# Selective scans: states summed by sixteen 32x32 tiles into four banks that y shares with the projection's scratch

## The chip, the core and the metric

The kernel runs on one core of a Trainium2 chip. The time is that of the whole program on the device, in microseconds (us). The kernel before takes 9509.47 us, the median of three runs (9506.33 to 9523.89).

## What is computed

Two layers of a "metaformer" on an input of 4 x 64 x 64 x 128, all in float32. Each layer adds a token mixer and then a channel mixer to x, each behind a layer norm. The change is in the token mixer of the second layer, a selective scan in four directions k over each image of L = 4096 positions, with 256 channels d (two halves of 128, called h) and 16 states n:

```
x_dbl = einsum('bkdl,kcd->bkcl', xs, x_proj_w)        # 8 rows for dt, 16 for B, 16 for C
dt = softplus(einsum('bkrl,kdr->bkdl', dts_r, dt_proj_w) + dt_proj_b)
h = h * exp(dt * A) + (dt * u) * B                     # for each position l, channel d, state n
y = einsum('bkdn,bkn->bkd', h, C)                      # the sum over the states
ys = ys + Ds * xs
y = ys[0] + ys[2] reversed + transposed(ys[1] + ys[3] reversed)
```

Directions 0 and 2 walk the rows of the image forward and backward, 1 and 3 the columns. After the scans y is normalized, gated and projected to 128 channels.

## The kernel before

The program runs its stages one after the other: attention, a recurrent layer solved by sweeps, the inputs of the scans (in_proj, a 3x3 convolution by 32x32 tiles at L950), the scans (L998 to L1485), their outputs, and a mixture of experts. Only the scans and the order of some weights are touched by the change.

**Windows, groups, tiles.** A sequence is cut into blocks of 125 positions. Four blocks make a window of W = 500 positions; there are 33 windows for each direction, 132 in all, walked in the order k = 2, 3, 0, 1. A window has four groups q of four states each, a group has a tile for each block. A tile holds 128 channels by two halves h by four states by 127 columns, 1016 columns in all. One DVE instruction scans a tile (L1297). There are 16 tiles in a window and 2112 scans.

**A step p of the schedule.** The order is written out by hand (the loop over p at the end of the function). In step p PE fills the addend db of tile p + 1 (L1273: eight matmuls of 32 rows that multiply dt * u by B into one of two double banks), ACT carries the last column of the states of tile p - 1 into the decays of the next tile of its group (L1318), DVE scans tile p, PE sums the states of a group that is done (L1348, at even p: two of four n each time), POOL multiplies the states of tile p by C (L1331) into a ring of twelve products, SP loads C for tile p + 5 (L1250), ACT computes exponentials of dt * A for coming groups (L1238), and one or two pieces of the projection of a coming window are put in.

**The projection** (`project`) is a generator whose pieces are tied to steps, from 40 to 10 steps ahead of its window. It has a scratch `mm` in PSUM, two banks, and uses it one after the other for: x_proj (L1142) and its copy xd (L1147); dt_proj (L1161), exp (L1172), a bound (L1175, L1177), ln (L1181) and the maximum that gives dt (L1186); the transposes of B (L1194), which DVE spreads on diagonals (b_diag, L1200); the transposes of dt * u (L1221), which ACT copies to dtu_t (L1223).

**y.** The sum over states is taken by PE: an identity of 64x64 times the products, for row halves r and channel halves h, four tiles of 64x64 with 500 columns that run together (L1348). Row half r goes to bank r, so y has two banks; in them partition 64 h + c, bank r stands for channel 128 h + 64 r + c. `add_other` (L1359) adds, by the same tiles, D * u in the backward directions and the y of the backward direction in the forward ones; k = 3 has nothing to add. `finish` (L1369) copies y on ACT, and SP writes it out. While y is open, each fill puts a matmul with zeros beside its pairs, into y, on a row group of 32 that the fill leaves idle (L1282, called a filler here): it adds nothing to y.

In the order of the halves that y has, the weights of the stages after it are laid out with channels exchanged (`turned`).

## Time and profile before

| | |
|---|---|
| median of three runs | 9509.47 us |
| the profiled execution | 9517.0 us |
| its span | 9515.2 us |
| scans, first to last start of L1297 | 3598 to 8847 us of the span |
| DVE scan L1297 | 2112 times, 4669.3 us busy |
| POOL products L1331 | 2112 times, 4457.4 us busy |
| ACT exponentials L1238 | 4224 times, 3017.5 us busy |
| PE sums L1348 | 16896 records of 64x500, 2019.2 us busy |
| granted PE clock in the scans, 4500 to 8700 us | 1.00 |

The page gives the busy time of each engine as a share of the span: PE is TensorE's matmuls (in float32 each matmul of the program is two records), PEld its weight loads, DVE VectorE, ACT ScalarE, POOL GpSimd, SP the queue that issues DMAs. Below stand groups of instructions by source line with their count, busy time and the mean of one, and then the idle time before them with the engine that ended it ("<-PE y L1348"). A timeline line has the start in us of the span, the time that the merged instructions took, engine, line, operation, result and operand, shapes and count. Matmuls that run together on different tiles of the array overlap in it.

### The profile page before, as it was taken

The page shows a single profiled execution, that of the slowest core. Times are in us where ns is not written, and L with a number is a line of the kernel's source. Part 1 is how long each engine was busy: PE and PEld are TensorE (multiplying, and loading weights), DVE is VectorE, ACT ScalarE, POOL GpSimd, SP SyncE. Part 2 cuts the span into 40 slices and gives each one's busy share as a digit, 9 for nine tenths or more (in the row PEclk, how much of TensorE's full clock was granted, in tenths as well). Part 3 has the DMA queues.
Part 4 walks back from the last instruction along what each step waited for, and adds up shares of the span by engine and source line. Part 5 has one row for each costly group of instructions (what it writes and reads, how often), then busy time and mean ns, then how long its engine had stood idle before and what let it go on. Part 6 is the DMA issues. An engine that isn't in the chain of part 4 may idle for free. (4 is left out here: it accounts for less than half of the span.)

```text
span 9515.2 us, 237518 instructions
## 1 busy us (share of the span) xinstructions
PE 8735.5 (92%) x102194; PEld 4329.6 (46%) x102194; DVE 8414.2 (88%) x5099; ACT 6880.6 (72%) x10398; POOL 5155.1 (54%) x2433
## 2 busy tenths in 40 slices
PE   7999999999988978999999999999999999999766
PEld 3333333333333335555555555555555555555223
DVE  6999999999978218999999999999999999999764
ACT  3888888888855457777777877877777777777321
POOL 0000000000001018999999999999999999999100
PEclk8999999999999988999999999999999999999887
DMA  4000000000011325666666556666666666666634
GB/s 171 31 8 34 10 8 35 8 8 10 8 60 62 123 121 156 170 171 171 170 167 160 160 160 158 160 168 171 171 171 171 171 170 171 171 171 165 228 116 182
DMA packets 530960, 1164.75 MB, mean 122 GB/s; under 512 B 76818, under 2 KB 444506, under 8 KB 502106
## 3 DMA queue, kind: packets, MB, share of 16 engines
q1 hardware_dynamic: 529882, 1149.30, 41.6%
q8 instruction: 807, 13.22, 0.6%
q14 instruction: 271, 2.22, 0.1%
HBM read 828.51 MB, written 182.15 MB: 106 GB/s over the span
## 5 line engine op out<-in xcount | busy, mean ns | idle before, releaser
L1297 DVE TENSOR_TENSOR_SCAN states<-decays,db 128x1016 f32<-128x1016 f32 x2112 | 4669.3, 2256 | 100.8 <-ACT decays L1318 61.5
L1331 POOL TENSOR_TENSOR products<-states,c_ring 128x1000 f32<-128x1000 f32 x2112 | 4457.4, 2152 | 219.9 <-PE y L1348 190.2
L1238 ACT ACTIVATE decays<-dt,a_logs 128x500 f32<-128x500 f32 x4224 | 3017.5, 714 | 90.4 <-DVE states L1297 4.2
L1273 PEld LDWEIGHTS db<-b_diag,dtu_t 32*128 32x128 f32 x16896 | 2051.3, 187 | 1607.0 <-DVE states L1297 1186.4
L1273 PE MATMUL db<-b_diag,dtu_t 32*128 32x128 f32 x16896 | 2429.8, 283 | 316.0 <-DVE states L1297 310.2
L1273 PE MATMUL db<-b_other,dtu_t 32*128 32x128 f32 x16896 | 2458.9, 284 | 0.0
L1282 PE MATMUL y<-zeros 32*128 32x128 f32 x14720 | 2122.4, 283 | 0.0
L1273 PEld LDWEIGHTS db<-b_other,dtu_t 32*128 32x128 f32 x16896 | 2050.1, 186 | 0.3 <-issue 0.2
L1348 PE MATMUL y<-products,ident 64*64 64x500 f32 x16896 | 2019.2, 592 | 1.1 <-POOL products L1331 1.1
L1282 PEld LDWEIGHTS y<-zeros 32*128 32x128 f32 x14720 | 1772.1, 186 | 0.0
L341 DVE TENSOR_TENSOR total<-total,ring 128x2048 f32<-128x2048 f32 x768 | 1706.9, 2285 | 32.5 <-ACT ring L303 31.8
masks.py:197 POOL MEMSET ident<- 128x128 f32 x6 | 1.2, 204 | 2915.1 <-SPq L180 2623.1
L303 ACT ACTIVATE ring<-sa 128x2048 f32<-128x2048 f32 (+3 forms) x667 | 1153.5, 1738 | 274.2 <-PE sa L288 262.6
L313 PE MATMUL av<-ring,v_at 128*32 128x256 f32 (+1 forms) x16128 | 1095.9, 388 | 6.2 <-ACT o L322 5.7
L1348 PEld LDWEIGHTS y<-products,ident 64*64 64x64 f32 x16896 | 541.3, 132 | 696.8 <-issue 568.3
L313 PEld LDWEIGHTS av<-ring,v_at 128*32 128x32 f32 x16128 | 421.4, 109 | 951.0 <-issue 749.0
L303 ACT ACTIVATE ring<-sb 128x1536 f32<-128x1536 f32 (+2 forms) x585 | 800.5, 1375 | 73.8 <-PE sb L288 63.9
L1318 ACT COPY decays<-states 128x8 f32<-128x8 f32 x2048 | 405.2, 198 | 536.3 <-DVE states L1297 520.0
L288 PE MATMUL sa<-q_at,k_at 32*128 32x512 f32 x4898 | 701.4, 641 | 20.3 <-issue 14.1
L288 PE MATMUL sb<-q_at,k_at 32*128 32x512 f32 x3294 | 624.1, 641 | 0.0
L288 PEld LDWEIGHTS sa<-q_at,k_at 32*128 32x128 f32 x4898 | 192.5, 183 | 354.4 <-issue 176.9
L338 DVE TENSOR_TENSOR total<-ring 128x2048 f32<-128x2048 f32 x128 | 288.6, 2287 | 66.7 <-ACT ring L303 66.4
(211 smaller groups left out, 7955.5 us busy)
## 6 DMA issues: line engine op xcount, KB each, us to landing
c_ring<-c_rows SPq DMA_DIRECT2D x2112, 250.0 KB, 4.6
b_other<-b_diag SPq DMA_DIRECT2D x264, 512.0 KB, 6.5
weights<-in_w SPq DMA_DIRECT2D x32, 1024.0 KB, 12.9
u<-u_r SPq DMA_DIRECT2D x60, 500.0 KB, 5.6
y_r<-sum SPq DMA_DIRECT2D x60, 500.0 KB, 4.2
u<-u_c SPq DMA_DIRECT2D x60, 500.0 KB, 5.7
y_c<-sum SPq DMA_DIRECT2D x60, 500.0 KB, 4.2
x<-x SPq DMA_DIRECT2D x96, 256.0 KB, 2.6
```

The lines of the kernel that those rows point to most:

```text
L288: nc.tensor.matmul(s[:, m, :], k[rows, tokens(t)], q[rows, chunk(chunk_state["c"])], start=True, stop=True,)
L303: nc.scalar.activation(ring[:, lo : lo + n, :], s[:, at : at + n, :], AF.Exp)
L313: nc.tensor.matmul(chunk_state["av"][rows, some], chunk_state["v"][:, t, rows], ring[:, at + i, some], start=t == 0, stop=t == NJ - 1 and ...
L338: nc.vector.tensor_add(total, sums[g - 2], w)
L341: nc.vector.tensor_add(sums[g % 2], sums[g % 2], w)
L1238: nc.scalar.activation(to, dt, AF.Exp, scale=scale)
L1273: nc.tensor.matmul(bank.rearrange("p (n t) -> p n t", n=4)[:, :, to : to + 32], v.dtu[rows, h, s, :], b[rows, s, 4 * self.q : 4 * self.q + ...
L1282: nc.tensor.matmul(y[:, idle // 2, :P], zeros[rows], zeros[rows], start=False, stop=False)
L1297: nc.vector.tensor_tensor_scan(order(self.slot(states)), order(self.slot(decays, shift)), order(self.db[:, SKIP + shift :][:, : 2 * LANE]) ...
L1318: nc.scalar.copy(self.edge(later.slot(decays), later.v.into), last)
L1331: nc.gpsimd.tensor_mul(to, h, c)
L1348: nc.tensor.matmul(to, ident[rows, rows], of, start=begins, stop=ends)
```

## The change

The sums, `add_other` and the layout of y go from 64x64 to 32x32 tiles: row groups r of 32 products rows, and column groups 2 h + j, where j is the half of the window (250 positions). Row group r writes bank r, so y now has four banks, 250 columns in each; partition 32 (2 h + j) + c, bank r stands for channel 128 h + 32 r + c. A block of sums has 32 matmuls of 250 columns instead of 8 of 500.

The scratch mm no longer has banks of its own: y is columns 0 to 249 and mm columns 256 to 511 of the same four banks (the two double banks of db hold the other four). The matmuls into mm no longer start a group of their own; they add onto places that ACT has set to zero. So three copies of zeros are put on ACT in each window's projection (`cleared`: after xd, after b_diag, after dtu_t; a fourth for the first two windows only), and the transposes become matmuls with an identity. x_proj and dt_proj are cut in two halves of 250 columns; dt_proj takes 64 rows of a weight tile that is zero beyond the 9 that matter. The fillers write into y as before, now into bank 1 or 2, that of their row group.

y is written to memory in natural channel order, by four DMAs for each piece of a window instead of one, and read back as `other` by one instead of four; the exchanged channel order of weights and norm goes away.

```diff
-    mm = ps.tile([P, ND, CH], F32, tag="mm", name="mm", bufs=1)
+    ym = ps.tile([P, 4, CH], F32, tag="ym", name="ym", bufs=1)
+    nc.vector.memset(ym, 0.0)
+    y, mm = ym[:, :, :WH], ym[:, :, CH // 2 :]
+    wide = mm[:, :, :WH]
+
+    def cleared(of):
+        nc.scalar.copy(of, zeros[:, 0:1].rearrange("p (r o) -> p r o", o=1).to_broadcast(list(of.shape)))
...
     def project(v):
...
-            nc.tensor.matmul(
-                x_ps[:, :W], w_x[:, h, k, :], v.u[:, h, :], start=h == 0, stop=h == ND - 1
-            )
+            for j in range(2):
+                nc.tensor.matmul(
+                    wide[:, 2 + j],
+                    w_x[:, h, k, :],
+                    v.u[:, h, j * WH : (j + 1) * WH],
+                    start=False,
+                    stop=h == ND - 1,
+                    skip_group_check=True,
+                )
...
+        cleared(wide[:, 2:])
...
         yield -17
+        if v in todo[:2]:
+            cleared(wide)
...
         yield -12
+        cleared(mm[:, 1:2, : NS * N])
...
         yield -10
-        nc.scalar.copy(v.dtu, turned)
+        nc.scalar.copy(v.dtu.rearrange("p h (j s) d -> p (h j) (s d)", j=2), mm)
+        yield -9
+        cleared(mm)
...
                     nc.tensor.matmul(
-                        y[:, idle // 2, :P], zeros[rows], zeros[rows], start=False, stop=False
+                        y[:, idle, :P],
+                        zeros[rows],
+                        zeros[rows],
...
+    def to_y(r, h, j):
+        c = 32 * (2 * h + j)
+        return y[c : c + 32, r, :]
+
+    def each_tile():
+
+        for r in range(4):
+            for h in range(ND):
+                for j in range(2):
+                    yield r, h, j
...
     def sum_of(pair, n):
...
-        for r in range(2):
-            rows = slice(HALF * r, HALF * r + HALF)
-            for h, g in enumerate(pair):
-                y = v.y[HALF * h : HALF * h + HALF, r, :W]
-                begins = q == 0 and n == 0
-                ends = q == Q - 1 and n == 3
-                of, to = window_of(products, rows, g, n, v.data.start, y)
-                nc.tensor.matmul(to, ident[rows, rows], of, start=begins, stop=ends)
+        for r, h, j in each_tile():
+            rows = slice(32 * r, 32 * r + 32)
+            of, to = window_of(
+                products, rows, pair[h], n, v.data.start, to_y(r, h, j), (2 * j, 2 * j + 1)
+            )
+            nc.tensor.matmul(
+                to,
+                ident32[rows],
+                of,
+                start=q == 0 and n == 0,
+                stop=q == Q - 1 and n == 3,
+                skip_group_check=True,
+            )
...
     def finish(v):
-        v.sum = work.tile([P, ND, W], F32, tag="sum", name="sum", bufs=1)
-        nc.scalar.copy(v.sum, v.y[:, :, :W])
+        v.sum = work.tile([P, 4, WH], F32, tag="sum", name="sum", bufs=1)
+        nc.scalar.copy(v.sum, y)
         for b, of, to in v.pieces:
-            nc.sync.dma_start(ys[b][v.k % 2][:, :, of], v.sum[:, :, to])
+            for j in range(2):
...
+                for h in range(ND):
+                    c = 32 * (2 * h + j)
+                    nc.sync.dma_start(
+                        ys[b][v.k % 2][:, h, at : at + end - first].rearrange(
+                            "(r c) t -> c r t", r=4
+                        ),
+                        v.sum[c : c + 32, :, first - j * WH : end - j * WH],
+                    )
```

## The prediction

> **What bounds the kernel now.** I read the page's first two parts, the busy time by stretch, the waits, and then one window of sixteen scans in the timelines of DVE, PE and ACT. Only the scans (3598 to 8856 us of the span) are touched.

> ```profile
> PE 8735.5 (92%) x102194; PEld 4329.6 (46%) x102194; DVE 8414.2 (88%) x5099; ACT 6880.6 (72%) x10398; POOL 5155.1 (54%) x2433
> 5500.00:6500.00 1000.00, 937.41 (x13125) 554.93 (x13124) 976.94 (x511) 792.88 (x1493) 969.59 (x458) 1.00 0.61 162
> POOL products L1331 <- PE y L1348: 143.3, 101, 1.7
> ACT sum L1369 <- PE y L1348: 120.6, 96, 1.9
> DVE dt L1186 <- POOL low L1177: 49.8, 100, 0.5
> DVE states L1297 <- ACT decays L1318: 42.2, 69, 1.0
> DVE states L1297 <- PE db L1273: 19.3, 100, 1.6
> ```

> The page makes PE the busiest. The second line (busy us of PE, PEld, DVE, ACT, POOL in 1000 us of scans) says that DVE, with 977, is the one with nothing left; PE's 937 holds fillers and modelled ends. The waits (us in total over 4000 to 8000, times, longest) show the small rest: three short waits of DVE, each in up to all of the 101 windows there, two of which begin with PE's sums L1348 (ACT's copy of y and POOL wait for them).

> ```profile
> 8537.62 13.15 DVE L1297 TENSOR_TENSOR_SCAN states<-decays,db 128x1016 f32<-128x1016 f32 x6
> 8551.38 4.48 DVE L1297 TENSOR_TENSOR_SCAN states<-decays,db 128x1016 f32<-128x1016 f32 x2 [0.62 <-ACT decays L1318]
> 8556.02 4.43 DVE L1297 TENSOR_TENSOR_SCAN states<-decays,db 128x1016 f32<-128x1016 f32 x2 [0.16 <-PE db L1273]
> 8560.95 0.68 DVE L1186 TENSOR_TENSOR dt<-mm,low 128x500 f32<-128x500 f32 x1 [0.50 <-POOL low L1177]
> ...
> 8577.50 13.15 DVE L1297 TENSOR_TENSOR_SCAN states<-decays,db 128x1016 f32<-128x1016 f32 x6
> ```

> Six scans back to back take 13.15 us, a step of (13.15 - 2.26) / 5 = 2.18. The window is 8577.50 - 8537.62 = 39.88. DVE's own work is 16 x 2.18 + two b_diag (1.15, 1.12 by their steps) + two dt (0.6) = 38.3. So only 1.5 us of a window is waiting: all that a faster PE can give back. By every sixteenth scan the windows take 39.9 in direction k=2, 39.2 in k=3 (no added other, L1359), 39.87 in k=0 and 1.

> **The change, part by part.** *The sums.* Now eight 64x64 matmuls, after it thirty-two 32x32 ones of half the columns.

> ```profile
> 6002.64 1.91 PE L1348 MATMUL y<-products,ident 64*64 64x500 f32 x16
> 6004.48 0.37 PE L1273 MATMUL db<-b_diag,dtu_t 32*128 32x128 f32 x1
> 3322.64 9.66 PE L950 MATMUL conv_ps<-xin,diag 32*32 32x512 f32 x286
> ```

> A block of sums holds PE for 6004.48 - 6002.64 = 1.84 us: 4 rounds of 0.42 (each matmul is two records of 500 columns; four tiles run together) and about 0.15 to switch tiles. The nearest row for sixteen 32x32 tiles is the convolution's: 9 taps in 9.66 us, less its last record's 0.6, is 1.0 us for each sixteen matmuls of about 507 columns; two passes at the sums' pace would be 0.85, so sixteen tiles cost about 0.17 more than their columns. For 250 columns: 2 x (0.42 + 0.17) + 0.1 = 1.28. [...] I take 1.25, near the row. PE is freed of 1056 x 0.59 = 620 us, and the added other shrinks by some 0.4 us in three windows of four. Against DVE's floor this can bring at most 1.5 us x 98 + 0.9 x 33 = 180 us.

> *The shared banks.* y takes columns 0 to 249 of four banks, the projection's scratch columns 256 to 511 of the same four. Before, mm and y had banks of their own, so ACT's copies from mm ran beside PE's fillers (L1282 writes y): the trace has them overlapping at no price. [...] PE takes matmuls in the program's order, so a waiting filler holds up all of PE behind it: the rest of its own fill, for which the next scan waits, then sums and projections. [...]

> *The clears.* Three copies of zeros on ACT per window, of 500, 64 and 1024 columns. Nearest rows: quarters 128x512 at 0.63, the carry L1318 at 0.2, dtu_t 128x1024 at 0.99. Together 1.85 us; ACT goes from 79% to about 84%. Off the path that is free; where a filler or a carry stands behind it, it is not (bounds: 0 if all is covered, 1.85 if none).

> ```profile
> 8543.63 0.99 ACT L1223 COPY dtu_t<-mm 128x1024 f32<-128x1024 f32 x1
> 8550.20 0.99 ACT L1369 COPY sum<-y 128x1000 f32<-128x1000 f32 x1 [1.48 <-PE y L1348]
> 8553.41 0.99 ACT L1172 ACTIVATE e<-mm 128x1000 f32<-128x1000 f32 x1
> 8554.52 1.04 ACT L1175 ACTIVATE low<-e 128x1000 f32<-128x1000 f32 x1
> ```

> *One window.* Slots are p modulo 16, time 0 is slot 0's scan; a fill takes 1.1 on PE (from 6004.48 its last records start at 6005.38, eight rounds of 0.11), and 0.85 from a released filler to its end (6 rounds and the last matmuls; 0.75 to 1.1), then 0.14 to the scan; decays take 0.74 each, a carry 0.2.
> - The first b_diag waited for a matmul ahead of the sums, now for the sums: fill 0.3 to 1.4, sums to 2.65, so 2.7 for 2.2: 0.5 lost.
> - xd (0.68) and its clear (0.63) follow b_diag, to 5.25; the filler goes at 5.3, the fill ends at 6.15, and the second b_diag now waits for it: 6.3 for 6.05, 0.25.
> - dtu_t now waits for the sums' end at 14.3 and ends at 15.3; fill to 16.2; slot 6's scan 16.35 for 16.15: 0.2.
> - ACT does a carry, two decays, then clears 1024 columns, to 18.0; filler, fill to 18.9, slot 7's scan 19.05 for 18.5: 0.55.
> - Three decays to 20.4, the copy of y to 21.4, the carry to 21.6; slot 8's scan 21.7 for 21.2: 0.5 (it is 0.6 to 0.7 now: the sums are no longer late, ACT is).
> - Three decays and the carry to 24.0; slot 9's scan 24.1 for 23.9: 0.2.
> - L1172 waited for w_dt's matmuls, now for the sums after them, at 24.65; exp, its reading, L1175 and the carry end at 26.9; slot 10's scan 27.0 for 26.3: 0.7.
> - dt no longer waits for POOL, but its second half waits for sums: 0.1.

> That is 3.0 us of waiting for 1.5, a window of 41.35. With the other added nothing changes, its 0.6 us ends before the clear does. Sum: 98 x (41.35 - 39.89) + 33 x (41.35 - 39.2) = 143 + 71 = 214 us. POOL (38.3 us of work in a window) stays below 41.35.

> *Small edits.* y goes out by four DMAs per piece for one, in runs of 1000 for 2000 bytes, and other comes in by one for four in k=0 and 1. The issues (0.56 us of SP each in the trace) stand before c_ring loads, which are put out five slots (12 us) ahead and land in 4.6: covered; without cover 3 x 0.56 per window in k=2, at most 55 us. w_dt with 64 rows for 9, w_x in halves, transposes as matmuls with an identity: the same columns through PE. Memsets and the clears before the first scan: about 6 us (0 to 15). Channel order costs nothing.

> The profiled execution took 9517.0 us (span 9515.2), 7.5 above the median of 9509.5. 9517 + 214 + 6 = 9737; against the median, 9730.

> **Rivals.** *Waiting doubles* (above), 9730, chance 0.68: for it the program's waits and DVE at 98%. [...] *Issue limits the sums*: a block of 2.1 makes those four steps 0.85 later each, 44.75 per window, 9509 + 131 x 5 = about 10170; chance 0.08; against it, bursts of three tiles start 7 ns apart in the fills. In between lie blocks of 1.5: +1 us, 9860. *PE was the bound and is freed, so it is faster*: if fillers are released within about 0.4 us of a fill's start, the waits L1348 causes go and no new ones come; DVE's floor of 38.3 gives up to 180 us, 9330; the wait counts of POOL and ACT on y speak for it, the nine waiting fillers against; chance 0.06. The rest, 0.04, is that the copies pass one another better than I laid out, within 0.2%.

> The range is 9540 to 9890: below it lie the faster case and the overlapping one, above it the issue limit, some 0.18 in all. 0.2% (19 us) is what a measurement tells from no change: faster 0.06, within 0.07, slower 0.87.

> **What will show it.** Right: L1369's successor and L1172 ended by PE y; fillers (L1282's) that idle for ACT; a window near 41.4; a block of sums of 1.2 to 1.35 us; DVE's share at 93%. DVE's waits should be named PE db and ACT decays, at slots 2, 6 to 10. Wrong: windows below 39.9, a block under 1.0 or above 1.8, a granted clock below 1.00 in the scans, or POOL waiting for c_ring.

## The result, and the profile after

The changed kernel takes 12818.5 us (median of four runs, 12758 to 12868), the kernel before 9514.1 us beside it: 1.347 times as long, 95% interval 1.339 to 1.355. The prediction was 9730 us, at most 9890. Its sign was right, its size wrong by 3090 us. The profiled execution of after has a span of 12864.0 us. Its busy times, its granted clock in 40 slices, and the stretch of scans that was shown of before:

```profile
PE 11458.5 (89%) x157898; PEld 7085.2 (55%) x157898; DVE 8534.2 (66%) x5099; ACT 7144.9 (56%) x10796; POOL 5202.1 (40%) x2433
...
PEclk8999999999866666666555555666666666666687
```

```profile
5500.00:6500.00 1000.00, 885.40 (x14316) 656.65 (x14284) 608.71 (x308) 514.48 (x958) 594.49 (x278) 0.62 0.39 100
```

DVE, which had 977 us of work in 1000, now has 609: it waits. PE is still busy for 885, but at a granted clock of 0.62 (the third number from the end), where before had 1.00. The PEclk row shows that this sets in with the scans and ends with them. Every sixteenth scan (131 distances) is 65.35 us apart on average, where before had 39.79: 25.56 x 131 = 3348 us, the whole difference of the two spans (12864.0 - 9515.2).

What the engines waited for, 4000 to 8000 us of after (us in total, times, longest):

```profile
DVE states L1346 <- PE db L1317: 1076.4, 591, 3.3
...
ACT e L1196 <- PE ym L1405: 301.8, 61, 5.0
ACT dtu_t L1266 <- PE ym L1405: 261.4, 61, 5.0
...
PE ym L1326 <- ACT ym L1075: 196.0, 121, 2.2
```

The first line was 19.3 us in before. Fillers (L1326) wait for ACT, as predicted. But look at who waited for the sums in the whole span. First before, all of it, then after (us, times):

```profile
who waited for it (us, times):
  POOL products L1331: 190.2, 130
  ACT sum L1369: 172.7, 125
```

```profile
who waited for it (us, times):
  POOL products L1380: 1045.4, 390
  ACT e L1196: 638.9, 130
  ACT dtu_t L1266: 558.9, 130
  ACT ym L1075: 453.4, 130
  DVE b_diag L1235: 325.3, 130
  DVE dt L1210: 289.8, 130
  ACT sum L1433: 285.9, 132
```

Five readers and clears of the projection's scratch, once in each window, stand behind blocks of sums from which they take nothing: they share their banks. One such place, in the order of start (the last brackets hold the idle time before the instruction and what ended it; L1196 is the exp that reads dt_proj's result):

```profile
7781.11 2.34 PE L1405 MATMUL ym<-products,ident 32*32 32x250 f32 x64
7781.32 2.27 DVE L1346 TENSOR_TENSOR_SCAN states<-decays,db 128x1016 f32<-128x1016 f32 x1 [1.70 <-PE db L1317]
...
7783.49 1.00 ACT L1196 ACTIVATE e<-ym 128x1000 f32<-128x1000 f32 x1 [4.95 <-PE ym L1405]
...
7784.63 0.57 PE L1326 MATMUL ym<-zeros 32*128 32x128 f32 x1 [0.46 <-ACT e L1196]
...
7786.45 2.27 DVE L1346 TENSOR_TENSOR_SCAN states<-decays,db 128x1016 f32<-128x1016 f32 x1 [2.85 <-PE db L1317]
```

Block of sums, reader, filler with the rest of its fill, scan: four links one after the other, 5.3 us from 7781.11 to 7786.45, for a step that takes 2.2 when nothing waits. And each PE link is long: the block takes 2.34 where at full clock it takes 1.47.

### The profile page after: what moved, and what is told of

The parts are those of the page before. It is cut to its first block, busy times and chain, and to the rows that moved or that the text cites. A ratio compares the mean times of both kernels' runs of the same rounds, so it can differ in the third digit from the quotient of the medians.

```text
span 12864.0 us, 349349 instructions
## 1 busy us (share of the span) xinstructions
PE 11458.5 (89%) x157898; PEld 7085.2 (55%) x157898; DVE 8534.2 (66%) x5099; ACT 7144.9 (56%) x10796; POOL 5202.1 (40%) x2433
## 5 line engine op out<-in xcount | busy, mean ns | idle before, releaser
L1326 PE MATMUL ym<-zeros 32*128 32x128 f32 x14720 | 3267.9, 387 | 925.2 <-ACT ym L1075 406.6
L1317 PE MATMUL db<-b_diag,dtu_t 32*128 32x128 f32 x16896 | 3978.7, 394 | 12.8 <-DVE states L1346 10.3
L1317 PE MATMUL db<-b_other,dtu_t 32*128 32x128 f32 x16896 | 3974.2, 394 | 0.0
L1317 PEld LDWEIGHTS db<-b_diag,dtu_t 32*128 32x128 f32 x16896 | 3267.4, 279 | 999.2 <-issue 759.0
L1326 PEld LDWEIGHTS ym<-zeros 32*128 32x128 f32 x14720 | 2790.4, 279 | 1180.5 <-ACT ym L1075 456.2
L1317 PEld LDWEIGHTS db<-b_other,dtu_t 32*128 32x128 f32 x16896 | 3263.0, 279 | 0.0
L1405 PE MATMUL ym<-products,ident 32*32 32x250 f32 x67584 | 2217.3, 555 | 0.3 <-POOL products L1380 0.3
L1405 PEld LDWEIGHTS ym<-products,ident 32*32 32x32 f32 x67584 | 1030.6, 128 | 607.0 <-issue 362.9
L288 PE MATMUL sa<-q_at,k_at 32*128 32x512 f32 x4898 | 701.4, 640 | 20.4 <-issue 14.1
L1235 DVE TENSOR_TENSOR b_diag<-ym,ident 128x1024 f32<-128x1024 f32 x264 | 323.2, 1224 | 424.9 <-PE ym L1405 325.3
L1210 DVE TENSOR_TENSOR dt<-ym,low 128x500 f32<-128x500 f32 x264 | 178.9, 678 | 629.3 <-PE ym L1326 311.0
```

What stands on the lines that cost most here:

```text
L288: nc.tensor.matmul(s[:, m, :], k[rows, tokens(t)], q[rows, chunk(chunk_state["c"])], start=True, stop=True,)
L1235: nc.vector.tensor_mul(v.b_diag[:, i : i + 2].rearrange("p s n t -> p (s n) t"), b_ps[:, i : i + 2] .rearrange("p s (n o) -> p (s n) o", o ...
L1317: nc.tensor.matmul(bank.rearrange("p (n t) -> p n t", n=4)[:, :, to : to + 32], v.dtu[rows, h, s, :], b[rows, s, 4 * self.q : 4 * self.q + ...
L1326: nc.tensor.matmul(y[:, idle, :P], zeros[rows], zeros[rows], start=False, stop=False, skip_group_check=True,)
L1405: nc.tensor.matmul(to, ident32[rows], of, start=q == 0 and n == 0, stop=q == Q - 1 and n == 3, skip_group_check=True,)
```

## The experiments

Two things had to be told apart: new waits, and a low clock. The trace records the granted clock as 1.00 or as 0.50, which is called half clock here. "Window" is the mean distance of every sixteenth scan, "half" the share of time in the scans at half clock, both over 111 windows (10 to 120, counted from 0). "Work" is what I counted in each trace: the columns that each matmul streams, times its share of the array's rows and columns, in 3.41 us (4096 would be the whole array at full clock without a break: eight records of 128x512, which start 0.43 us apart at full clock and 0.85 at half, L118 of before). "Idle" is PE's longest idle time there. Work is not independent of the clock: at half clock PE streams half as many columns in the same time (125 columns of the sums take 0.41 us at full clock and 0.83 at half, E11 below). E1, E3, E4 and E11 were run once, the others twice or more.

```
kernel                                   us      window  work  PE busy  idle  half
before                                  9514.1    39.7   2721   0.94    1.7   0.00
E4 before, no fillers                   9528.4    39.8   2407   0.94    1.7   0.01
E1 before, half sums                    9406.0    39.0   2116   0.84    3.2   0.08
E7 before, half sums, no fillers       11376.1    53.9   1301   0.98    1.0   0.91
E6 before, fillers in scratch           9777.7    41.8   2654   0.94    1.5   0.03
E8 the same, half sums                  9600.4    40.6   2104   0.91    1.5   0.16
E16 as E6, light ties                  11367.5    54.0   2060   0.89    1.6   0.20
E17 as E8, light ties                  11507.2    54.6   1568   0.90    1.6   0.52
after                                  12818.5    65.6   1312   0.89    2.2   0.76
E2 after, two fillers                  11049.3    51.5   1908   0.84    2.2   0.25
E3 after, no fillers                   11767.0    57.0   1293   0.94    2.7   0.78
E10 after, fillers where they are free 10739.7    49.3   1673   0.89    3.6   0.40
E9 after, sums of 32x64                12159.8    59.8   1894   0.87    2.2   0.28
```

### The clock: E1 to E4, E7

The first theory, A, was that the clock follows the work done in the array: half sums and waits leave too little. Its rival B: idle PE behind the new waits trips it.

E1 is before, with sums of two blocks of four:

```diff
-                nc.tensor.matmul(to, ident[rows, rows], of, start=begins, stop=ends)
+                half = slice(0, NB) if begins else slice(2 * (n % 2), 2 * (n % 2) + 2)
+                nc.tensor.matmul(
+                    to[:, half],
+                    ident[rows, rows],
+                    of[:, half],
...
```

> The kernel before, with its own banks for mm and y, but each sum L1348 takes only two of the four blocks (250 of 500 columns; the first one of a window takes all), so part of y is left out: PE's useful work per block is halved as in the change, with no new wait anywhere. Theory A (the granted clock follows how much of the array works within a 3.4 us stretch: columns x rows x columns of the tile): a pair of slots brings 1536 from fills and 1000 from sums for 2000, so the clock falls in some stretches: mean clock in the scans 0.80 to 0.98, 9450 to 10500 us. Theory B (PE standing still behind the new waits lets the clock fall; less work alone does not): clock 1.00 and 9330 to 9500 us.

E2 is after with a second filler in each place; E3 and E4 are after and before without any (`if False:` for the filler's condition).

```diff
-                if summed[-1]:
-                    rows = slice(32 * idle, 32 * idle + 32)
+                for r in (idle, (idle + 2) % 4) if summed[-1] else ():
+                    rows = slice(32 * r, 32 * r + 32)
                     nc.tensor.matmul(
-                        y[:, idle, :P],
+                        y[:, r, :P],
...
```

> The changed kernel with a second filler beside the first, in the fourth row group that a fill leaves idle: the waits are all there, a fill brings 1024 instead of 768 of array work. Theory A: the clock comes back to 0.95 to 1.00 in the scans, and the slots run as the prediction laid them out: 9620 to 9850 us. Theory B (idle time behind waits): the gaps are as long as before, so the clock stays at 0.6 and the time at 12500 to 13100.

> The changed kernel without any filler: fills no longer wait for ACT or DVE in their middle, and there is less array work. Theory A: half clock nearly throughout (0.50 to 0.58 in the scans); fills of 1.7, sums of 2.3 and the projection give some 54 to 62 us per window, 11400 to 12500 us, so PE's pace at half clock is the bound. Theory B: the gaps go with the waits, the clock is back above 0.9, 9400 to 9900 us.

> The kernel before without its fillers. Theory A: a pair of slots still brings 1024 + 2000, in the poorest 3.4 us about 2000, above the some 1450 where the clock changed in the changed kernel's trace: clock 1.00, 9480 to 9560 us. Rival (the fillers themselves hold the clock, because they keep a further row group busy at all times): the clock falls below 0.8 and the time is over 10500.

E1 took 9406.0 us, E2 11049.3 (ratio 1.161, 1.158 to 1.165), E3 11767.0, E4 9528.4. B's numbers fail for E2 and E3: more work beside the same waits raised the clock and saved 1770 us; the fillers' waits removed, work with them, left it low. A has the times of E3 and E4 right and E2 wrong: E2 has 1908 of work, a clock mostly full, and still windows of 51.5. E1 fell between the two, A's clock at B's time. It also answers what a shorter block is worth without sharing: 1.1% less time than before in one run. Its 51 windows (of all 131) without half clock take 38.31 us on average, DVE's own 38.3.

E7 joins E1 and E4: half sums, no fillers, no new wait.

> Before with the sums of 250 of 500 columns (part of y is left out) and without fillers: the array work of a window is the same as in the changed kernel without fillers (some 1770 columns of the whole array in 3.4 us if a window takes 40 us), but no wait is new. Theory W: clock 0.85 to 1.00 in the scans, windows of 38.3 to 41 us, 9350 to 9650 us. Rival C: the clock falls as in the changed kernel without fillers (0.6), windows above 44 us, over 10200 us.

11376.1 us (1.196; 1.193 to 1.200), the line of C, the rival that held the array work alone to be enough. The stretch 5500 to 6500 of E7, of E1 and of E4:

```profile
5500.00:6500.00 1000.00, 979.54 (x7736) 681.06 (x7734) 747.60 (x384) 606.42 (x1130) 736.43 (x344) 0.54 0.46 119
```

```profile
5500.00:6500.00 1000.00, 833.86 (x13259) 582.73 (x13251) 977.16 (x515) 803.39 (x1510) 978.37 (x462) 0.96 0.63 165
```

```profile
5500.00:6500.00 1000.00, 935.52 (x10268) 547.47 (x10264) 973.60 (x509) 793.12 (x1494) 966.61 (x457) 0.99 0.61 161
```

PE is busy for 980 of 1000 us in E7 and has a clock of 0.54; in E1 it is busy for 834 and has 0.96. So PE's busy time alone is not what the clock goes by here. Either cut of work alone keeps it; both together lose it. The low clock then thins the work further, by an estimate: at half clock E7's windows take 54 us, so its 20566 units of work a window come to 1301 in 3.41 us, while in windows of 39.8 they would be 1760.

### The waits: E5, E6, E8, E10

E6 brings into before one thing of the change: the fillers go into the scratch. (dt_proj also takes 64 rows, with zeros, as in after; so it is in E8 and E14 to E17.)

```diff
-                        y[:, idle // 2, :P], zeros[rows], zeros[rows], start=False, stop=False
+                        mm[:, idle % 2, :P], zeros[rows], zeros[rows], start=False, stop=False,
...
```

With fillers among the values under way in the scratch, E6's output is off by a relative 0.031; E8 and E14 to E17 have them there too.

> Before, with one thing of the change alone: the fillers write into the projection's scratch (the bank that matches after's) in place of y's banks, so that they wait for ACT and DVE as in after, while the sums stay 64x64 and the array work of a window stays what it was (the dt projection takes 64 rows with zeros in place of 25 so that the tiles can stand beside each other). Theory W: the scans get late, windows of 42 to 48 us, PE has empty stretches but 64x64 sums around them, clock 0.85 to 1.00, 9850 to 10900 us. The size of waits in the prediction (3 us a window in place of 1.5): windows of 41 to 41.5 us at clock 1.00, 9700 to 9780 us. Rival C: clock 1.00, since the array work is there. If the empty stretches alone hold the clock down: clock below 0.8 and over 11000 us.

> Before with two things of the change and nothing else: the sums of 250 of 500 columns (part of y is left out; array work of a window as in after) and the fillers in the projection's scratch (waits as in after). Alone the first gave 9406 us and the second 9778 us. Theory I (the clock is decided by the array work per stretch of 3.4 us, so that less work and new waits, each harmless alone, together put many stretches below the threshold, and the low clock then holds itself): clock in the scans below 0.85, windows above 46 us, 10500 to 12500 us. Rival S (the two add up, and the rest of after's time is of the 32x32 tiles or the clears): 9406 - 9509 + 9778, about 9675 us, clock above 0.93, 9550 to 9900 us.

E6 took 9777.7 us (1.028; 1.025 to 1.031). Its 84 windows (of all 131) without half clock are 41.22 us on average: what the prediction had for the whole change, and below theory W's 42 to 48. E8, with half sums too, took 9600.4 (1.010; 1.007 to 1.013): rival S has its time right, the two nearly add up (9675), and theory I, that their meeting is enough, falls. Less work and waiting fillers do not make after.

E5 and E10 take the waiting fillers out of after and double the others. This is E10's list of places:

```diff
+                late = self.p % 16 in (0, 4, 5, 6, 8, 9, 12, 13, 15)
+                for r in (idle, (idle + 2) % 4) if summed[-1] and not late else ():
...
```

> After, with no filler in the nine fills per window whose first filler was seen to wait (tiles 2, 3, 4, 6, 7, 10, 11, 13, 14 of 16) and two fillers in each of the other seven. No part of the computation changes: fillers add zeros. Theory W (the waits of the fillers behind the shared banks make the scans late and leave PE empty; the empty stretches bring the clock down, and the low clock then does the rest): windows of 16 scans from 42 to 46 us, clock in the scans above 0.9, 9850 to 10450 us. Rival C (the clock goes by the average array work alone, and the sums' half work is what is missing): the nine bare fills are like those of the kernel without fillers, clock 0.55 to 0.7 in the scans, windows of 53 to 57 us, 11300 to 11900 us.

> After, with two fillers in each fill whose first filler did not wait, and none in the nine of 16 where it did. The earlier kernel of this kind took the places in the order of the fills for the tiles' numbers, which are two higher, and so left most waits in; here the numbers are right. Theory I: the fillers' waits are gone, but nine fills hold no filler: the average is some 2070 columns of the whole array in 3.4 us at windows of 40 us, between the kernel that fell (1770) and the one that mostly held (2115): clock 0.75 to 0.97, windows of 40 to 50 us, 9600 to 11000 us. Rival: the waits of the fillers are not what delays the scans, and the time stays where the earlier one was, above 11200 us.

E5 took 11319.4 us (1.190) and tells little: its list was of places in the order of fills, two below the tiles' numbers, so most waits stayed. E10 took 10739.7 us (1.130; 1.126 to 1.133), within theory I's range and the best of after's kin, and still 1230 us above before: with no filler that waits, its windows with 0.2 to 0.3 of half clock are 47.0 us.

### The sums' own sharing: E9, E12 to E17

E9 gives the sums of after their array work back.

```diff
+    nc.vector.tensor_copy(padded[:, 32:64], ident32)
...
-                ident32[rows],
+                padded[rows, 32 - 32 * j : 96 - 32 * j],
```

> After with its sums by tiles of 32 rows x 64 columns: the identity has 32 zero columns beside it, so that each matmul also adds zeros to the other half's partitions. Nothing of the computation changes; the array work of the sums is that of before again (2000 columns of the whole array a block in place of 1000), their instructions, banks, clears and waits are after's. Theory I: the clock is back at 0.93 or above in the scans, and what remains is the waits at full clock and a block near before's 1.84 us: windows 41.5 to 46 us, 9750 to 10450 us. Rival T (the many small instructions, not their array work, bring the clock down): clock below 0.8, over 11500 us.

12159.8 us (1.279; 1.275 to 1.283) at a clock of 0.87. Theory I missed the time, and its rival T, whose time it is, missed the clock: most of the clock came back, the time did not. With PE busy for only 0.87 and DVE for two thirds (2973 of 4500 us), this is waiting; its block is 2.27 us, and readers that stand behind it wait longer.

So theory Q: readers wait for blocks of sums, fillers for readers. E12 issues the projection ahead of the sums in after, E13 in E10.

```diff
             if p in at:
                 at[p].scan()
+            projections(p)
             sums(p)
...
-            projections(p)
```

> After, with the projection's steps of a turn issued ahead of the turn's sums in place of behind them. Nothing of the computation changes. Theory Q (both ways of the sharing make a chain: the projection's reader on ACT or DVE waits for a whole block of sums that was issued ahead of it in its banks, and the next fill's first filler waits for the reader, so that block, reader and fill follow each other; the low clock comes of the PE time lost and stretches each link): the readers no longer stand behind the block, though the block now stands behind the reader: windows of 44 to 57 us, clock 0.65 to 0.95, 10200 to 11800 us. Rival C (the array work decides, the order of issue matters little): 12500 to 13100 us.

> The same swap in the kernel that has two fillers in the seven fills that did not wait and none in the nine others (10740 us without the swap, windows of 47 to 51 us). Theory Q: of the two sides of the chain one is shortened and the other gone: windows of 41 to 47 us, 9700 to 10650 us. Rival C: no change within 150 us of 10740.

E12: 12095.3 us (1.272), 720 below after, but above Q's range and below C's; E13: 11554.3 us (1.215), 815 above E10, where Q expected a gain. The swap turns the wait round: the sums then wait for readers and clears, 432 us in E12 from 4000 to 8000 us, where after has no such wait. The largest of these in E12:

```profile
PE ym L1405 <- ACT ym L1075: 198.4, 132, 2.7
```

Neither of the two orders of issue gets rid of it.

E14 to E17 leave before as it is and tie its sums to the scratch: a small matmul of zeros into each bank of the scratch, ahead of each block and behind it. In E14 and E15 it has 128x128 and 32 columns, in E16 and E17 64x64 and 4 columns.

```diff
+        def tie():
+            for bank in range(ND):
+                nc.tensor.matmul(
+                    mm[:HALF, bank, :4], zeros[:HALF, :HALF], zeros[:HALF, :4],
+                    start=False, stop=False,
...
+                tie()
                 sum_of(pairs[g], turn)
                 sum_of(pairs[g], turn + 1)
+                tie()
```

> Before with the fillers in the projection's scratch (9778 us) and, in addition, two matmuls of zeros of 32 columns ahead of each block of sums and two behind it, one into each bank of the scratch: the sums themselves stay 64x64, whole, and in banks of their own, but now wait for the scratch's readers, and the readers wait for the end of the block, as in after. The zeros meet values of the projection under way, so its output is not the reference's. Theory Q: the chain of block, reader and fill is there with all the array work: windows of 45 to 53 us at a clock above 0.9, 10250 to 11300 us. Rival C: what little is added (some 0.2 us a block) hides: 9750 to 9900 us.

> The same ties in the kernel with sums of 250 of 500 columns and the fillers in the scratch (9600 us; part of y is left out): array work of after, and both ways of after's waits, with 64x64 tiles and no clears. Theory Q with the clock behind it: this is most of after: clock 0.55 to 0.85 in the scans, windows of 48 to 66 us, 10700 to 12900 us. Rival C: clock 0.9 and 9600 to 9850 us. Rival T (the 32x32 tiles or the clears hold the rest of after's time): 9600 to 10300 us.

> As the kernel with ties and whole 64x64 sums, with lighter ties: 4 columns of a 64x64 tile, the tile form of the sums, in place of 32 columns of the whole array. The first ties took 1.2 us a block, 10 us of TensorE a window, so that TensorE's own work (48 us a window) was part of that window of 61.4 us. Theory Q: with ties that cost below 0.3 us a block, TensorE's own work is some 40 us a window and what the chain of block, reader and fill adds stays: windows of 46 to 56 us, clock above 0.85, 10400 to 11900 us. Rival (the ties' own time was the cause): 9800 to 10150 us.

> The light ties with sums of 250 of 500 columns (part of y is left out) and the fillers in the scratch: the array work of after's sums and both ways of after's waits, without 32x32 tiles, clears or split products. Theory Q and the clock: clock 0.5 to 0.8 in the scans and windows of 50 to 66 us, 11000 to 12900 us, so that after's time needs nothing of the 32x32 form. Rival T (the 32x32 form, with 64 instructions a block and 1.40 us in place of 1.01, or the clears, are needed for it): clock above 0.85 and under 10500 us.

E14 took 12714.8 us (1.337), E15 13875.2 (1.459), both above Q's ranges, but these ties take 1.1 us a block at full clock where nothing waits (2.96 with them, 1.84 without), so part of it is their own. The light ones take 0.4 (2.23). E16 took 11367.5 us (1.195; 1.192 to 1.199), E17 11507.2 (1.210; 1.206 to 1.214), both within Q's ranges. E16 against E6 differs in the ties alone: 1590 us. One of its 51.3 us windows, and the first b_diag in it with its neighbours:

```profile
8256.50:8307.80 51.30, 45.20 (x590) 30.43 (x589) 39.01 (x21) 31.48 (x60) 38.30 (x19) 0.97 0.49 133
```

```profile
8256.47 2.27 DVE L1299 TENSOR_TENSOR_SCAN states<-decays,db 128x1016 f32<-128x1016 f32 x1 [0.37 <-ACT decays L1320]
8260.93 1.22 DVE L1201 TENSOR_TENSOR b_diag<-mm,ident 128x1024 f32<-128x1024 f32 x1 [2.19 <-PE mm L1451]
8262.07 2.26 DVE L1299 TENSOR_TENSOR_SCAN states<-decays,db 128x1016 f32<-128x1016 f32 x1
```

And the same place in E6, without ties:

```profile
7004.72 8.96 DVE L1299 TENSOR_TENSOR_SCAN states<-decays,db 128x1016 f32<-128x1016 f32 x4
7013.64 1.22 DVE L1201 TENSOR_TENSOR b_diag<-mm,ident 128x1024 f32<-128x1024 f32 x1
```

With ties b_diag waits 2.19 us for the tie (L1451) behind the block, and so on average over the 111 windows of the table; without them, in E6, it follows its scan at once in each of these. E16's 36 windows (of all 131) with less than 0.1 of half clock are 51.3 us on average: at nearly full clock and with all the array work, the sharing by the sums costs 10 us a window above E6, of which the ties' own time is about 3 at most (8 x 0.39). E17 has the same sharing with after's sum work: half clock rises from 0.20 to 0.52, and what the shorter block saves is lost again.

### The block of sums: E11

```diff
-                to,
+                to[:, :1],
                 ident32[rows],
-                of,
+                of[:, :1],
```

> After with each matmul of the sums cut to one of its two blocks of 125 columns (half of y's sums are left out). If the block of sums is limited by the issue of its 64 instructions, it stays at 1.40 us at full clock (22 ns each) with half of the columns; if by the columns, it is near 0.75 us. The clock in the scans will be low, since still less array work is done (0.5 to 0.6, windows above 55 us if the block stays, above 48 us if it halves).

12365.1 us. The block with 125 columns in E11, at half and then at full clock, and with 250 columns in after, at full and then at half clock:

```profile
7011.14 1.51 PE L1405 MATMUL ym<-products,ident 32*32 32x125 f32 x64
7019.38 1.06 PE L1405 MATMUL ym<-products,ident 32*32 32x125 f32 x64
```

```profile
10179.12 1.47 PE L1405 MATMUL ym<-products,ident 32*32 32x250 f32 x64
10186.75 2.34 PE L1405 MATMUL ym<-products,ident 32*32 32x250 f32 x64
```

By starts of successors (0.07 less than these spans) the block takes 0.99 and 1.40 us at full clock, 1.44 and 2.27 at half. So 125 columns cost 0.41, or 0.83 at half clock, and 0.58 to 0.61 stays at either: neither issue nor columns alone. Sixteen tiles do run together (64 records of 125 columns by sixteens are 500 column times, 0.41 us), and 64 records add 9 ns each at either clock. The 64x64 form fits the same sum: E1's 1.00 to 1.07 and before's 1.84 differ by about 0.8 for 250 columns in each of four rounds and leave some 0.2 for 16 records.

## Why the prediction was wrong, point by point

Three terms of the sum failed: the waits, forecast at 3.0 us a window for 1.5, the transposes, put at nothing, and durations that were all taken at full clock. In their place E2 shows windows some 10 us longer than before's with most of the half clock gone, where the forecast had 1.6, and after itself spends 0.76 of the scans at half clock.

**What bounds it.** DVE with a floor of 38.3 us a window, and at most 180 us to gain: right. E1 found the floor at 38.31.

**The block of sums.** Forecast 1.25; measured 1.40 at full clock. The mechanism, columns and a fixed part, was right; the fixed part was 0.58 and not 0.42. A small miss. The rival of 2.1, with the four steps of a window that hang on the sums' ends 0.85 us later each, took the convolution's pace, 9.06/286 = 32 ns, for 64 records; no run shows it: E11 showed 9 ns a record beside the time of the columns. A block of its columns alone (0.83 us) no run shows either.

**The shared banks.** The forecast took it that fillers wait for ACT and DVE on the scratch, and ACT and DVE for whole blocks of sums or fills, although their columns differ. Before shows none of these waits, from which the 3.0 us are added up; after does, where the forecast put them: from 4000 to 8000 us fillers (L1326) waited for ACT's clears 121 times, 196.0 us, and exp (L1196) for blocks of sums 61 times, 301.8 us. The filler that came 0.46 us late at 7784.63 held up the matmuls behind it: the rest of its fill follows from 7784.64. Whether the chip needs these waits, which are the program's, is not shown. "That is 3.0 us of waiting for 1.5" is the first term that failed. The window that it gave for the whole change, 41.35, is what E6 shows for the waiting fillers alone, 41.22. For readers behind whole blocks of sums it had losses of 0.1 to 0.7 us; E16 shows some 10 us a window for them. The schedule kept before's start times and added each loss to them: the first b_diag's block was to end 2.65 us after the scan, and 0.5 us to be lost. In E2, where this place ran at full clock in all 111 windows of the table, that block starts a microsecond later than laid out, since PE comes to the fill late, from transposes (L1222) and x_proj (L1150), and the block ends at 3.84:

```profile
4164.62 0.96 PE L1222 MATMUL ym<-ident,b_rows 16*128 16x16 f32 x8
4165.51 1.11 PE L1150 MATMUL ym<-u,w_x 128*128 128x250 f32 x4
4167.66 1.48 PE L1405 MATMUL ym<-products,ident 32*32 32x250 f32 x64
4169.17 1.22 DVE L1235 TENSOR_TENSOR b_diag<-ym,ident 128x1024 f32<-128x1024 f32 x1 [1.63 <-PE ym L1405]
```

The scan started at 4165.29 there, so b_diag comes at 3.88 for the forecast 2.7. A loss of one slot was never carried into the next, nor from DVE back to PE.

**"The same columns through PE"**, the step that cost the transposes as matmuls at nothing, was wrong. The trace of before has 8 records for the transposes of dt * u, after has 16. First before, then E2, which has after's projection and shows it at full clock:

```profile
4014.59 1.09 PE L1221 MATMUL mm<-ident,quarters 128*128 128x128 f32 x8
```

```profile
5013.73 2.05 PE L1257 MATMUL ym<-ident,quarters 128*128 128x128 f32 x16
```

To their successor they take 1.98 for 1.06 us, and those of B 0.89 for 0.29, at full clock. That is 1.5 us of PE a window, and those of B stand in the path of the first b_diag above. At half clock the 16 records take 3.71.

**The clears.** 0.58 + 0.21 + 1.01 = 1.80 us for 1.85: right in size. How much they add to the chain was not taken apart.

**The clock.** Every duration of the sum was taken at full clock. That was no step of the working, only named among the signs of being wrong ("a granted clock below 1.00 in the scans"), and it is the larger part. E2 is after with more zeros: its 49 windows (of the table's 111) with 0.1 to 0.2 of half clock take 49.6 us on average, where after has 65.6 and before 39.7. So with most of the half clock gone, 16 of after's 25.9 us are gone too, and 10 stay, part of them for the half clock that is left. What the waits and PE's longer links would cost at full clock is an estimate: a line through E2's windows has 2.2 us for each tenth of half clock, so 0.76 of it is about 17 us and the waits some 9; one through after's own has 3.1, which leaves some 2. Neither kernel has a window with less than 0.1 of half clock, so the split is not shown closer than that. It is not the same in every kernel: E16 has 11.6 us above before with less than 0.1 of half clock. Cause and effect are not separate either: after's longer windows hold 1312 of work in 3.41 us for before's 2721, the clock falls after stretches with little of it (1008 on average in after, the last section), and at half clock PE's links are longer (a block of sums 2.27 us for 1.40), which stretches the window.

**The rivals.** None was near. All of them, and the forecast, took the work that falls away as a gain or as nothing. It can be counted ahead: 31654 units a window before, less 1000 for each of eight blocks, and some 1500 more for the transposes, dt_proj's 64 rows and what else changed, make after's 25193. In a window of 41.35 us that would be 2080 in 3.41 us, near E1's 2116, which mostly held its clock: so the count alone would have warned, not decided.

**What stays open.** E17 has both ways of the sharing and half sums and takes 54.6 us a window, after 65.6. Transposes, clears, the split projections, 0.4 us more a block and the 32x32 form are what is left between them; which of these holds the 11 us is not shown, and no kernel that adds one of them to E17 was run. No kernel with 32x32 sums in banks of their own was tried either. None of these kernels that does the whole computation beats before.

## What to carry to other kernels

Before letting two uses share a PSUM bank, list for each reader which matmuls it will now stand behind, and for each matmul which reader; then lay the links end to end, carry every delay on, and do it with durations at half clock too (the waits for blocks of sums cost some 10 us a window in E16; a block takes 2.27 us at half clock for 1.40). Cutting array work on an engine that is not the bound isn't free: count columns times tile area per 3.4 us before and after, since zeros that looked like waste (the fillers, and what larger tiles multiply by zero) may be what keeps the clock up: before could lose either with little harm to its clock (half clock 0.01 of the time in E4, 0.08 in E1), but not both (0.91 in E7). In a sum of small tiles count a fixed time per record (here some 9 ns in 32x32 tiles), and matmuls in place of transposes as two records each in float32 (16 records and 1.98 us here for 8 and 1.06).

## What the runs showed of the hardware

```
          full stays full   full falls     half rises      half stays
before    2724 (2036)       one: 1248      one: 2192       none
E1        2227 (1710)       1246 (1662)    1597 (1479)     1275 (1553)
E7        1956 (1896)       1248 (1582)    1551 (1320)     1256 (1512)
after     2040 (1704)       1008 (1268)    1649 (1422)     1161 (1480)
E2        2249 (1576)        957 (1469)    1562 (1383)     1234 (1630)
PE busy, after   0.94       0.52           1.00            0.92
PE busy, E7      0.87       0.66           1.00            1.00
```

Counted so, each record at its start, the border lies at about 1450 to 1650 of 4096, 0.35 to 0.40 of the whole array, in each of these kernels. All 19 kernels together, with each record spread over its time, make it sharper: over the table's 111 windows of each, one border at 1446 tells for 99.1% of 18070 stretches at full clock whether the clock falls next, and one at 1520 for 98.3% of 14894 at half clock whether it rises. PE's busy share does 94.2% of the first at best; at half clock it tells nothing (always guessing "stays" has 82.1%). Columns times rows without the tile's width do 94.2% and 82.6%, so the whole area counts. These borders are fitted to the same stretches that they sort. At half clock a PE that is never idle does at most half of the array's 4096 (128x512 records start 0.85 us apart for 0.43), and 32-row fills and 32x32 sums less than that, so a kernel of small tiles can be too thin to climb back, as E7 was: its stretches that stayed at half had PE busy all the time.

**A low clock does not stretch everything.** In after a fill goes from 1.10 us at full clock to 2.01 at half, and a block of sums from 1.40 to 2.27, less than twice: some 0.6 us of it for 64 records does not scale (0.58 at full clock and 0.61 at half, E11).
